# A cross-attention kernel: queries of batches 2 and 3 by seven block products, more warm-up products, and subtractions moved on Pool and VectorE

## Chip, core and metric

The kernel runs on one core of a Trainium2 chip. A core has a matrix engine (TensorE, PE in the profile, with its weight loads as PEld), VectorE (DVE), ScalarE (ACT), Pool (GpSimd) and SyncE (SP), which here only issues transfers. All data is float32. The metric is the device time of one launch in microseconds (us); the median of 3 runs before the change is 906.13 us (905.66 to 906.14). The profile is of one further execution, in the trace of which every instruction has a start and a duration.

## What is computed

For each of 16 batches there are 100 rows of hidden states `x` (640 wide, 8 heads of 80) and 722 rows of context (384 wide), of which the last 4 are tokens for a second attention. Cut to what matters:

```python
query = hidden_states @ Wq
keyt, valt = enc @ Wk, enc @ Wv              # enc: 718 context rows
hs = _mha(query, keyt, valt)                 # main attention
ca_q1 = jnp.einsum('btc,th->bch', ca, Wq_ca)[:, indices, :]
ca_hs1 = _mha(ca_q1, residual, residual)     # over the 100 rows of x
ca_q2 = ca_hs1 @ Wq
ca_hs2 = _mha(ca_q2, ca @ Wk_ca, ca @ Wv_ca) # over the 4 tokens
out = (hs + ca_hs2) @ Wout + b_out + residual
```

## The kernel before

The loop at the end of the kernel runs over the batches `b`. In batch b the values of b and the keys of b+1 are computed; the main attention of b and the second attention of b and b+1 run around them. The order on every engine is the program's order (a manual schedule), so an instruction waits in its engine's queue behind everything that the program issues to this engine before it.

**Values and keys** (`Values`, `Keys`, both from `Blocks`). The product of 3 x 3 blocks of context with 3 x 2 blocks of weights is made by 15 block products instead of 18, from sums of context blocks that Pool makes (`enc_sums`, L497). Each step of `vv.go(n)` or `kk.go(n)` issues n block products (L431 values, L462 keys) into banks of PSUM named A to E, and after each product reads the bank: the first time into a block of the output by a copy of ScalarE (L404), later by an addition of VectorE (L402). The next product into the same bank waits for that read. Bank C of the keys takes a place that bank C of the values must have left.

**Softmax of the main attention.** `scores` leaves three tiles `st[0]` to `st[2]`. `Maximum` finds row maxima in steps on VectorE (transposes, reductions) and spreads them into a tile `over`; `top.go(n)` takes n of its steps. `subtract(i)` (L1517, VectorE, two operands in SBUF, 120 x 1600) and `exponential(i)` (L1525, ScalarE) follow.

**The second attention** (`Second`). `scores1` makes `e1` on Pool, for each of 4 tokens a multiply (L980) and, from the second on, an addition (L987). `softmax1(n)` takes n steps of a `Maximum` over `e1`; with `fine` that maximum is cut into smaller steps; when all are taken and `hold` isn't set, VectorE subtracts (L1006). `scores2` ends with a subtraction of 100 x 32 elements on the engine it is given (L1062; VectorE in batch 1, Pool from batch 2 on). `softmax3` makes `p2` on Pool (L1076). `values2` makes, on Pool, for each token a multiply of the token's value row `vb` (L1091) and an addition (L1098); the transfers of the rows of tokens 2 and 3 are issued on SP after the multiplies of tokens 0 and 1 (two buffers).

**Queries.** Two batches share one product with `Wq`. `queries` (L541) does it plainly: for each of 5 chunks of 128 columns, 5 products of 128 x 128 weights with 200 columns. `Queries.make` does it for batches 4 and 5 and on: the fifth chunk plainly (L632), the first four as a 2 x 2 block product by seven block products instead of eight (L599), with remainders, into banks named a to f. Its first sums of inputs and weights are made on Pool by `Queries.sums` (L593, six subtractions), a further one in between (L656). They lie in the unused part of the context tile of batch b+2. Between the products `make` issues steps of the second attention's maximum (`between`), products of the fifth keys chunk (`chunk.go`, L742) and what is given in `steps`. It needs the block (1, 0) of `Wq` to hold the sum of two blocks, which VectorE makes in place (L1826) at the end of batch 1.

**Output.** The output rows are taken in tiles of 128 rows; some pairs of tiles are complete after batches 2, 5, 7, 10 and 12 (`PAIRS`, keyed by the batch). They are projected by `project_pair` (L1259) in the batch after, that is 3, 6, 8, 11 and 13, where `last.b in PAIRS`: the "output batches" below. There Pool adds the bias to the rows of `x` (L1133, two additions) and makes two sums (L1240), and VectorE reads the banks of the product (L1270). `MIXED` are the batches 3, 5, 7, 9, 11 and 13, in which the queries of the next pair are made by `Queries.make`.

**Start.** While the first data are loaded, 21 small products of a zero tile run on TensorE (L1333); the first real ones are `first_values` (L372).

## Time and profile before

| | us |
|---|---|
| median of 3 runs | 906.13 |
| the profiled execution, whole | 907.72 |
| its span (first to last instruction) | 906.0 |
| busy in the span: PE | 900.3 (99%) |
| busy: DVE | 720.6 (80%) |
| busy: POOL | 712.8 (79%) |
| busy: ACT | 461.9 (51%) |

Rows of the timeline have start, duration, engine, line of the kernel, operation, output and inputs, shape, the number of instructions merged into the row, and in brackets the idle time before it with what ended it. A product in float32 leaves two records. [...] Rows of a source line give minimum, median and maximum duration in ns.

### The profile page before, as it was taken

The numbers are of one execution on the slowest core, as the hardware profiler recorded it, in microseconds if no ns is written. First come the engines' busy times: TensorE is split into PE (matmuls) and PEld (weight loads), VectorE is DVE, ScalarE is ACT, GpSimd is POOL, SyncE is SP. The second block draws the span as 40 slices with busy tenths as digits, with TensorE's granted clock in tenths as the row PEclk, the third lists the DMA queues.
The fourth block names the chain that finished last, engine by engine and source line by source line (L and its number), as shares of the span: only waits on it lengthen the run. The fifth ranks groups of instructions, "written<-read, shape, count | busy, mean of one in ns | idle before, by whom it ended". The sixth has DMA issues, their size and how long they took to land.

```text
span 906.0 us, 28486 instructions
## 1 busy us (share of the span) xinstructions
PE 900.3 (99%) x12200; PEld 748.1 (83%) x12200; DVE 720.6 (80%) x1278; ACT 461.9 (51%) x917; POOL 712.8 (79%) x684
## 2 busy tenths in 40 slices
PE   9999999999999999999999999999999999999998
PEld 6898889787797878878798787988879788797866
DVE  3669796999849898786987869788984899848893
ACT  2344543747437564644737446375742747437451
POOL 8689998787868889696896959958897688976633
PEclk9999999999999999999999999999999999999999
DMA  8723111132301212230122301203130031310111
GB/s 292 264 70 92 36 58 43 37 95 53 112 4 52 80 41 67 54 105 32 53 56 53 106 34 52 56 25 107 54 83 32 24 107 53 98 32 24 62 47 38
DMA packets 50627, 63.00 MB, mean 70 GB/s; under 512 B 13594, under 2 KB 37850, under 8 KB 50500
## 3 DMA queue, kind: packets, MB, share of 16 engines
q1 hardware_dynamic: 48852, 59.18, 21.4%
q8 instruction: 96, 1.57, 0.7%
q10 hardware_dynamic: 1024, 1.15, 0.4%
q0 software_dynamic: 624, 0.85, 0.3%
q14 instruction: 31, 0.25, 0.1%
HBM read 55.59 MB, written 5.57 MB: 68 GB/s over the span
## 4 chain that ended last, share of the span: by engine, by line
PE 94%; DVE 5%; ACT 0%; DMA 0%; issue 0%; DVEq 0%
PE a_ps L1806 12%; PE s_ps L781 12%; PE v_psA L431 10%; PE k_psA L462 8%; PE v_psB L431 8%; PE k_psB L462 6%; PE o_ps L1259 5%; PE k_psA L742 4%; PE v_psC L431 3%; PE k_psC L462 3%; PE v_ps L372 2%; PE q_ps L599 2%; PE q_ps L541 2%; PE v_psD L431 2%; PE v_psE L431 2%; PE k_psE L462 1%
## 5 line engine op out<-in xcount | busy, mean ns | idle before, releaser
L980 POOL TENSOR_TENSOR e<-ca,g 100x800 f32<-100x800 f32 x64 | 97.9, 1540 | 90.9 <-ACT kT L404 67.4
L1806 PEld LDWEIGHTS a_ps<-vs,st 120*64 120x64 f32 (+3 forms) x3072 | 119.0, 124 | 10.1 <-issue 0.7
L497 POOL TENSOR_TENSOR enc<-enc 128x240 f32<-128x240 f32 x144 | 113.2, 796 | 14.2 <-DMA enc<-in_enct 7.2
L1806 PE MATMUL a_ps<-vs,st 120*64 120x81 f32 (+3 forms) x3072 | 122.8, 233 | 0.0
L1517 DVE TENSOR_TENSOR st<-st,over 120x1600 f32<-120x1600 f32 x48 | 116.6, 2431 | 0.0
L431 PE MATMUL v_psA<-wv_sb,enc 128*120 128x320 f32 x352 | 109.3, 433 | 0.0
L1098 POOL TENSOR_TENSOR hs<-hs,hs 100x640 f32<-100x640 f32 x48 | 94.8, 1975 | 3.8
L987 POOL TENSOR_TENSOR e<-e,e 100x800 f32<-100x800 f32 x48 | 93.4, 1945 | 3.8
L462 PE MATMUL k_psA<-enc,wk_sb 128*128 128x240 f32 x384 | 95.2, 371 | 0.2 <-DVE kT L402 0.2
L1091 POOL TENSOR_TENSOR hs<-vb,p 100x640 f32<-100x640 f32 x64 | 90.6, 1426 | 3.8 <-DMA vb<-va_d 1.5
L431 PE MATMUL v_psB<-wv_sb,enc 128*120 128x320 f32 x296 | 91.9, 433 | 0.0
L1525 ACT ACTIVATE st<-st 120x1600 f32<-120x1600 f32 x48 | 73.9, 1539 | 23.5 <-DVE st L1517 23.2
L462 PEld LDWEIGHTS k_psA<-enc,wk_sb 128*128 128x128 f32 x384 | 71.5, 190 | 16.4 <-issue 1.2
L431 PEld LDWEIGHTS v_psA<-wv_sb,enc 128*120 128x120 f32 x352 | 64.2, 183 | 25.0 <-DVE vs L402 0.5
L1529 DVE TENSOR_TENSOR most<-most,st 120x800 f32<-120x800 f32 x64 | 68.0, 1063 | 14.3 <-ACT st L831 13.2
L462 PE MATMUL k_psB<-enc,wk_sb 128*128 128x240 f32 x320 | 77.9, 366 | 0.0
L781 PE MATMUL s_ps<-qp,kT 64*56 64x100 f32 (+1 forms) x3072 | 73.3, 248 | 0.0
L431 PEld LDWEIGHTS v_psB<-wv_sb,enc 128*120 128x120 f32 x296 | 54.1, 183 | 21.8 <-DVE vs L402 0.4
L781 PEld LDWEIGHTS s_ps<-qp,kT 64*56 64x56 f32 (+1 forms) x3072 | 67.0, 130 | 5.5 <-issue 4.2
L837 ACT COPY st<-s_ps 120x800 f32<-120x800 f32 x64 | 49.8, 830 | 38.7 <-PE s_ps L781 38.5
L1166 ACT COPY hsT<-turned_hs 32x160 f32<-32x160 f32 (+7 forms) x244 | 67.7, 278 | 3.0
L462 PEld LDWEIGHTS k_psB<-enc,wk_sb 128*128 128x128 f32 x320 | 60.9, 190 | 7.9
(213 smaller groups left out, 1905.9 us busy)
## 6 DMA issues: line engine op xcount, KB each, us to landing
vb<-va_d SPq DMA_DIRECT2D x62, 250.0 KB
enc<-in_enct SPq DMA_DIRECT2D x30, 240.0 KB
enc<-in_enct SPq DMA_DIRECT2D x15, 360.0 KB
xT<-in_xt SPq DMA_DIRECT2D x8, 500.0 KB
rest<-in_enct SPq DMA_DIRECT2D x31, 120.0 KB
xn<-in_x SPq DMA_DIRECT2D x11, 320.0 KB
out<-xn SPq DMA_DIRECT2D x11, 320.0 KB
ca<-in_cas SPq DMA_DIRECT2D x16, 156.2 KB
```

What stands on the lines that cost most here:

```text
L431: nc.tensor.matmul(at[0][j][:KN, : H // 2], a_form(self.enc, f)[:, j * KN : (j + 1) * KN], wv_there.get(f, wv_sb[:, W_AT[f]]), start=first ...
L462: nc.tensor.matmul(at[:, i * KT : (i + 1) * KT], wk_sb[:, W_AT[f], i], a_form(self.enc, f), start=(first and i == 0), stop=last, skip_grou ...
L497: nc.gpsimd.tensor_tensor(out, left, right, op)
L781: nc.tensor.matmul(s_ps[at][k0:k1, cols], w, rhs, start=not begun & {(at, k) for k in range(k0, k1, 32)}, stop=last, skip_group_check=True,)
L980: first = nc.gpsimd.tensor_tensor(to, self.ca[:, t, :].unsqueeze(1).to_broadcast([S, NH, S]), g[:, :, t].unsqueeze(2).to_broadcast([S, NH, ...
L987: made = nc.gpsimd.tensor_tensor(e, e, to, ALU.add)
L1091: first = nc.gpsimd.tensor_tensor(to, self.vb[t][:S].rearrange("p (h d) -> p h d", h=NH), p2[:, :, t].unsqueeze(2).to_broadcast([S, NH, D] ...
L1098: nc.gpsimd.tensor_tensor(sums, sums, to, ALU.add)
L1517: return nc.vector.tensor_tensor(st[i], st[i], top.over[:KN].unsqueeze(1).to_broadcast([KN, 2, ROWS]), ALU.subtract,)
L1525: nc.scalar.activation(st[i], st[i], AF.Exp, scale=SCALE)
L1529: most_now = nc.vector.tensor_tensor(most[:KN], most[:KN], st[i][:, u], ALU.max)
L1806: nc.tensor.matmul(a_v[lo:hi, h % 4], st[i // 2][: KEYS[i], i % 2, h * S + lo : h * S + hi], block(i, h // 4)[: KEYS[i], h % 4], start=(i ...
```

## The change

- 28 small products at the start instead of 21.
- In batch 1 the second attention's `scores1` for batch 2 comes behind `scores2` of batch 1, for all four tokens, and the subtraction of `scores2` is on Pool as in the other batches.
- In batch 1 `values2` makes tokens 0 and 1 where it made all four; tokens 2 and 3 follow within the queries.
- The queries of batches 2 and 3 are made by `Queries.make`, without a keys chunk between its products; its `sums` stand on Pool behind the load of the bias; the in-place sum of `Wq` blocks moves to the end of batch 0; the maximum of batch 2's second softmax is taken in fine steps between the products instead of in one piece before them.
- In the output batches one `vv.go(1)`, a values product with VectorE's eviction, comes ahead of `subtract(0)` and `exponential(0)` instead of behind them, so that `subtract(0)` and `subtract(1)` stand next to each other on VectorE.

```diff
--- before.py
+++ after.py
@@ -626,7 +626,8 @@
             def add(bank, g, m):
                 nc.vector.tensor_tensor(q(g, m), full(bank), q(g, m), ALU.add)
 
-            chunk.go(2)
+            if chunk:
+                chunk.go(2)
             for ch in range(HC):
                 for k in (0, 64):
                     nc.tensor.matmul(
@@ -643,14 +644,16 @@
                 )
             between(2)
             steps[0]()
-            chunk.go()
+            if chunk:
+                chunk.go()
             self.product(a, w(0, 0), v(0, 0), True)
             nc.scalar.copy(q(0, 0), full(a))
             steps[1]()
             self.rest(c, 0, 0, True)
             self.product(c, w(0, 1), v(1, 0), False)
             add(c, 0, 0)
-            chunk.go()
+            if chunk:
+                chunk.go()
             between(1)
             self.product(a, self.w2, self.t2, False)
             nc.gpsimd.tensor_tensor(self.w2, w(0, 1), self.w2, ALU.subtract)
@@ -660,7 +663,8 @@
             self.product(e, w(1, 1), self.t4, False)
             nc.scalar.copy(q(1, 0), full(e))
             add(a, 1, 0)
-            chunk.go()
+            if chunk:
+                chunk.go()
             self.product(b, self.w3, self.t3, True)
             add(b, 1, 0)
             between(1)
@@ -997,7 +1001,7 @@
                     e1,
                     f"1_{self.b}",
                     after - 1 in PAIRS or after in PLAIN,
-                    after in (*MIXED, *PLAIN) or after - 1 in PAIRS,
+                    after in (1, *MIXED, *PLAIN) or after - 1 in PAIRS,
                 )
             if self.less:
                 return
@@ -1329,7 +1333,7 @@
     idle = small.tile([P, P], F32, tag="idle", name="idle")
     nc.vector.memset(idle, 0.0)
     idle_ps = psum("idle_ps")
-    for _ in range(21):
+    for _ in range(28):
         nc.tensor.matmul(
             idle_ps[:32, :32], idle[:, :32], idle[:, :32], start=True, stop=True
         )
@@ -1603,12 +1607,16 @@
                     nc.gpsimd.tensor_tensor(o, left, right, ALU.subtract)
             elif last.b - 1 in PAIRS:
                 nc.gpsimd.tensor_tensor(wout2[:, 0], wout2[:, 0], forms[0], ALU.add)
-            second.scores1(seen, range(T - 1))
+            if b > 1:
+                second.scores1(seen, range(T - 1))
             top.go(3)
             kk.go(3)
             vv.go(3)
-            now.scores2(nc.vector if b == 1 else nc.gpsimd)
-            second.scores1(None, range(T - 1, T))
+            now.scores2(nc.gpsimd)
+            if b > 1:
+                second.scores1(None, range(T - 1, T))
+            else:
+                second.scores1()
             now.load(behind=seen)
             last.load(seen)
             top.go(1)
@@ -1625,12 +1633,17 @@
             if last.b in PAIRS:
                 last.sums()
             later = range(T - 1, T) if b in MIXED or last.b in PAIRS else range(0)
+            if b == 1:
+                later = range(2, T)
             now.values2(None, range(T - len(later)))
             vv.go(2)
             kk.go(1)
+            if last.b in PAIRS:
+                vv.go(1)
             subtract(0)
             exponential(0)
-            vv.go(1)
+            if last.b not in PAIRS:
+                vv.go(1)
             subtract(1)
             vv.go(1)
             kk.go(2)
@@ -1652,6 +1665,9 @@
                 nc.gpsimd.dma_start(out=bias, in_=bout[0].partition_broadcast(P))
             if not mixed:
                 second_next, enc_next = loads()
+            if b == 1:
+                first_queries = Queries(p + 1, xT_at[0], enc_next[0])
+                first_queries.sums()
             if b + 2 < B:
                 m_next = load_m(b + 2)
             late = mixed and last.b not in PAIRS
@@ -1672,8 +1688,6 @@
                     )
             if not mixed and last.b in PAIRS:
                 now.values2(None, later)
-            if b == 1:
-                second.softmax1(8)
         else:
             room = enc_tile("spare").rearrange("p f k -> p (f k)")
             spare.extend(room[:, i * H : (i + 1) * H] for i in range(2))
@@ -1704,8 +1718,17 @@
         if b % 2 and b + 1 < B:
             xT, tiles = xT_at[0], queries_tiles(p + 1)
             if not mixed:
-                for n, get in enumerate((psum1, psumk, psum1, psumk, bank)):
-                    queries(p + 1, xT, tiles, n, get)
+                first_queries.make(
+                    tiles,
+                    None,
+                    lambda n=9: second.softmax1(n, True),
+                    (
+                        lambda: None,
+                        lambda: None,
+                        lambda: now.values2(None, later),
+                    ),
+                )
+                second.softmax1()
             else:
                 if last.b in PAIRS:
                     second.softmax1()
@@ -1822,7 +1845,7 @@
         if b + 2 < B:
             second_next.products()
             second_next.copy()
-        if b == 1:
+        if b == 0:
             nc.vector.tensor_tensor(
                 wq_block(1, 0), wq_block(1, 0), wq_block(1, 1), ALU.add
             )
```

## The prediction

> **What bounds the kernel now.** I read the chain of waits first, then the timelines by engine around every place that the change touches.
>
> ```profile
> PE 94%; DVE 5%; ACT 0%; DMA 0%; issue 0%; DVEq 0%
> ```
>
> TensorE (PE in the rows) carries 94% of the chain, so a product less is worth its own time and anything that makes TensorE wait costs in full. VectorE (DVE), ScalarE (ACT) and Pool count only where they are late. The places where TensorE waits today are few. Two of them matter here, in batch 1 and in batch 13:
>
> ```profile
> 113.03 1.24 PE L431 MATMUL v_psA<-wv_sb,enc 128*120 128x320 f32 x4
> 114.48 1.05 PE L462 MATMUL k_psA<-enc,wk_sb 128*128 128x240 f32 x4 [0.20 <-DVE kT L402]
> 115.55 1.08 PE L462 MATMUL k_psE<-enc,wk_sb 128*128 128x240 f32 x4
> 131.98 8.65 PE L541 MATMUL q_ps<-xT,wq_sb 128*128 128x200 f32 x50
> 140.56 0.43 PE L742 MATMUL k_psC<-enc,w_sums 128*64 128x120 f32 x4
> ...
> 772.77 0.97 PE L462 MATMUL k_psB<-enc,wk_sb 128*128 128x240 f32 x4
> 774.08 1.08 PE L462 MATMUL k_psC<-enc,wk_sb 128*128 128x240 f32 x4 [0.34 <-DVE vs L402]
> ```
>
> In batch 1 a values block is followed after 1.45 us (114.48 - 113.03) and the keys block behind it after 1.07. Undisturbed, the steps are 1.08 and 0.81, as batch 3 shows below (231.51 - 230.43, 232.32 - 231.51). TensorE lost 0.37 + 0.26 = 0.63 us waiting for VectorE. In batch 13 a keys block of 0.81 took 1.31, so 0.50 was lost. The plain queries of batches 2 and 3 take 140.56 - 131.98 = 8.58 us.
>
> **The change part by part.** All times are of the profiled execution, 907.72 us with a span of 906.0; it lies 1.59 above the median of 906.13, and I add the differences to the median.
>
> *Warm-up products.*
>
> ```profile
> 1.13 2.45 PE L1333 MATMUL idle_ps<-idle 128*32 128x32 f32 x42 [1.13 <-DVE idle L1330]
> 3.63 1.42 PE L372 MATMUL v_ps<-wv_sb,rest 128*120 128x320 f32 x2
> 7.25 0.77 PE L372 MATMUL v_ps<-wv_sb,rest 128*120 128x320 f32 x2
> ```
>
> 42 records (21 products) take 2.45 us, so 7 more take 0.8 and would end at 4.4 where real work now begins at 3.63. Two records of the first real product take 1.42 us against 0.77 at 7.25: until about then the array runs at half rate, and loads of weights still wait for data. Ends: 0 (the gap is filled by waits anyway) and +0.8; I take **+0.3**, because a delay before 7.25 shrinks by half when the rate doubles. [...]
>
> *The second softmax's subtraction in batch 1, from VectorE to Pool, and the score products behind it.*
>
> ```profile
> L1062 POOL TENSOR_TENSOR e<-s,mx x14: 238/243/249, 170.9 to 872.1; 100x32 f32<-100x32 f32 x14
> L1062 DVE TENSOR_TENSOR e<-s,mx x2: 1222/1249/1276, 74.1 to 110.8; 100x32 f32<-100x32 f32 x2
> ```
>
> VectorE loses an instruction of 1.25 us just ahead of its evictions; Pool gains 0.24. The 0.63 us of TensorE waiting should go, for the eviction that TensorE waited for at 114.48 (0.20 by the row's own count, the rest in the loads behind it) comes some 1.25 sooner. Bounds: 0 and -0.63.
>
> *Seven block products for eight.*
>
> ```profile
> 246.75 0.86 PE L599 MATMUL q_psA<-xT,wq_sb 128*64 128x100 f32 x16
> 247.43 1.20 PE L599 MATMUL q_ps<-xT,wq_sb 128*64 128x100 f32 x24
> ```
>
> In batch 3 one block product (16 records) takes 247.43 - 246.75 = 0.68 us, a remainder (8 records) half, 0.34. The new queries are the fifth chunk (a fifth of 8.58, 1.7), seven products (4.8) and four remainders (1.4): 7.9 us for 8.58, a gain of 0.7 if nothing is waited for. But three of the products need sums that Pool makes first, and this is where I expect the loss. Pool's queue of batch 1 now, with VectorE's subtractions beside it:
>
> ```profile
> 110.52 3.03 POOL L980 TENSOR_TENSOR e<-ca,g 100x800 f32<-100x800 f32 x2
> ...
> 127.51 2.50 POOL L1091 TENSOR_TENSOR hs<-vb,p 100x640 f32<-100x640 f32 x2
> 130.09 1.54 POOL L1098 TENSOR_TENSOR hs<-hs,hs 100x640 f32<-100x640 f32 x1
> ...
> 138.98 0.60 POOL L1652 DMA_DIRECT2D bias<-in_bout  x1
> ...
> 123.10 2.72 DVE L1517 TENSOR_TENSOR st<-st,over 120x1600 f32<-120x1600 f32 x1
> 130.44 2.88 DVE L1517 TENSOR_TENSOR st<-st,over 120x1600 f32<-120x1600 f32 x1
> ...
> L593 POOL TENSOR_TENSOR enc<-xT x12: 596/608/613, 240.6 to 791.3; 128x200 f32<-128x200 f32 x12
> L593 POOL TENSOR_TENSOR enc<-wq_sb x6: 1262/1268/1281, 241.9 to 789.5; 128x512 f32<-128x512 f32 x6
> ```
>
> A large subtraction of VectorE takes about 1.8 us alone (226.80 below); here it takes 2.88, because it begins at 130.44 and runs only once Pool's addition has ended at 131.63. The two exclude each other. After the change Pool starts the score products some 0.5 us later (it first does the 0.24 subtraction, which waits for VectorE), and since TensorE and VectorE are 0.63 ahead, the third subtraction comes before the addition of 130.09 instead of behind it and holds it for 1.7. The addition ends near 131.63 + 0.5 + 1.7 = 133.8. Behind it in Pool's queue stand the bias load (0.6), then the six sums, 4 x 0.61 + 2 x 1.28 = 5.0. The first weight sum, third in order, is there at 134.4 + 2 x 0.61 + 1.27 = 136.9, the second at 139.4, and its update (1.28) at 140.7. TensorE, at 131.35 after the fifth chunk's 1.7, one product, one remainder and one product, is at the first of them at 134.75 and waits 2.1 us. It waits again for the other two, and the queries end 0.68 + 0.34 + 0.68 = 1.7 after Pool's last sum, at 142.4 instead of 140.56: **+1.8**, whatever TensorE gained before. There is no keys chunk between these products to fill the gap, as there is in batch 3.
>
> Behind the queries VectorE has two copies of the maximum, two adds and the scores' subtraction before it can evict the keys chunk that TensorE goes on with; that subtraction can meet a Pool multiply of 1.25 (half of the 2.50 row). 0 to 0.8, taken **+0.5**. Batch 1 in all **+2.3**; bounds +0.1 (the third subtraction does not hold Pool) and +4 (one hold of 1.7 more).
>
> *Moved and costed at nothing.* The in-place sum of the query weights goes from the end of batch 1 to the end of batch 0, where VectorE idles 2.65 us for ScalarE; uncovered it would cost 1.0. Pool's later work in batch 1 (two value products, five key rows, the sums of the next context, the output weights' differences) shifts by some 8.5 us (0.5 + 1.7 + 5.0 + 1.3); before batch 2 Pool idles 6.24. The rest, some 2 us, makes batch 3's scores late; the exclusion could then slow the maxima by up to 1.5, which is in the range. SP's two loads of token values for tokens 2 and 3 are issued after the same multiplies as before and are used later.
>
> ```profile
> 99.03 0.99 DVE L1541 TENSOR_TENSOR most<-st 128x800 f32<-128x800 f32 x1 [2.65 <-ACT st L837]
> ...
> 162.37 3.04 POOL L980 TENSOR_TENSOR e<-ca,g 100x800 f32<-100x800 f32 x2 [6.24 <-ACT kT L404]
> ```
>
> *Batches 3, 6, 8, 11 and 13: an eviction ahead of the first large subtraction.* Batch 3 now:
>
> ```profile
> 222.41 3.67 DVE L1517 TENSOR_TENSOR st<-st,over 120x1600 f32<-120x1600 f32 x1
> 226.00 0.88 DVE L402 TENSOR_TENSOR vs<-v_psC,vs 120x320 f32<-120x320 f32 x2
> 226.80 1.81 DVE L1517 TENSOR_TENSOR st<-st,over 120x1600 f32<-120x1600 f32 x1
> 228.53 0.81 DVE L402 TENSOR_TENSOR vs<-v_psB,vs 120x640 f32<-120x640 f32 x1
> ...
> 221.35 3.05 POOL L1133 TENSOR_TENSOR xn<-xn,bias 128x640 f32<-128x640 f32 x2
> 226.14 0.73 POOL L1240 TENSOR_TENSOR sum<-hsT 128x256 f32<-128x256 f32 x1
> ...
> 223.96 1.24 PE L431 MATMUL v_psC<-wv_sb,enc 128*120 128x320 f32 x4
> 230.43 1.24 PE L431 MATMUL v_psB<-wv_sb,enc 128*120 128x320 f32 x4
> 231.51 0.97 PE L462 MATMUL k_psC<-enc,wk_sb 128*128 128x240 f32 x4
> 232.32 1.24 PE L431 MATMUL v_psA<-wv_sb,enc 128*120 128x320 f32 x4
> ```
>
> The first subtraction stands 3.67 us, until Pool's two additions end at 224.40. That is what makes TensorE wait in batch 13, since the eviction behind it frees the bank for the next keys block. With the eviction first, that wait goes (at most 0.5 in batch 13, and I allow as much for 11). But the block to be evicted starts at 223.96, so its eviction ends at about 225.7, VectorE idles until then, and the two subtractions come back to back. By then Pool, no longer held, is in its second sum (to 226.1). The first subtraction runs from 226.1 to 227.85. What happens between two adjacent subtractions batch 15 shows:
>
> ```profile
> 883.08 1.81 DVE L1517 TENSOR_TENSOR st<-st,over 120x1600 f32<-120x1600 f32 x1
> 884.81 2.90 DVE L1517 TENSOR_TENSOR st<-st,over 120x1600 f32<-120x1600 f32 x1
> ...
> 883.42 2.61 POOL L1091 TENSOR_TENSOR hs<-vb,p 100x640 f32<-100x640 f32 x1 [0.27 <-DMA vb<-va_d]
> ```
>
> Pool's multiply, waiting since 883.42, goes between them and ends 1.14 after the first; the second then ends 1.68 later. So in batch 3 the second ends at 227.85 + 1.14 + 1.68 = 230.7, and the values eviction behind it at 231.4 instead of 229.34 (228.53 + 0.81). TensorE wants that bank at 230.43: it had 1.1 us to spare, and now waits **1.0**. By the same walk over rows for which there is no room here, batch 8 has the same spacing (1.0) and batch 6 a little more room (0.7); in 11 and 13 the wait that goes about pays for the new one (0). Sum **+2.7**; bounds -1.0 (only the gain) and +9 (below).
>
> Then the third subtraction, two microseconds later than now, meets Pool's additions again, ahead of the read that frees a bank of the output product:
>
> ```profile
> 235.81 0.45 DVE L1270 TENSOR_TENSOR xn<-o_ps,xn 128x320 f32<-128x320 f32 x1
> 236.90 2.32 PE L1259 MATMUL o_ps<-wout,hsT 128*128 128x320 f32 x8
> ```
>
> The read ends 0.64 us before TensorE needs it. VectorE is 2.0 late, TensorE 1.0, so at least 0.4 is lost in batch 3, and 1.9 if a Pool addition (1.54) goes first. Over five batches 0 to 4; I take **+2.0**. Sum: 0.3 + 2.3 + 2.7 + 2.0 = +7.3, 906.13 to **913.4** (915.0 for an execution like the profiled one).
>
> [...]
>
> **The rivals.**
>
> [...]
>
> [...]
>
> *Pool is not held in these stretches, and the change gains.* This decides in batch 1, on Pool: TensorE comes to the product that needs the second weight sum at 134.75 + 0.68 + 0.34 + 0.68 = 136.45, so the six sums must begin by 131.4. Without holds of about 1.7 from three subtractions they would begin 5.1 sooner than 134.4, at 129.3, and nothing waits: -0.63 - 0.7 there. Without holds the five batches only gain their 1.0, and the total is 0.3 - 1.3 - 1.0 = -2.0: 904.1. Against it stand the rows 2.72 and 2.88 in this very stretch.
>
> **How the numbers follow.** About what a measurement of this kernel can tell from no change is 0.2%, 1.8 us: 904.3 to 907.9. The forecast has 0.61, with its own range 909 to 917 from the bounds of its terms; the slower rival 0.12; the one near 907.7 0.14; the faster one 0.13. Slower 0.73, same 0.14, faster 0.13. The range, 904.6 to 917, holds the forecast and the rival at 907.7 and leaves out the faster one and half of the slowest.
>
> **What would show it.** In batch 1: the pair of blocks at 113.03 steps at 1.08 and 0.81, and the query products show waits for Pool's sums, some 2 us ahead of the first weight sum. In batches 3, 6 and 8: two adjacent large subtractions, the second above 2.5 us with a Pool instruction between them, and TensorE waiting for a values eviction. In 11 and 13 the wait of the keys block is gone. I am wrong if the queries of batch 1 run 7.9 us without a gap, or if the values blocks of batches 3 and 8 keep their 1.08 steps.

## The result and the profile after

The changed kernel takes 920.69 us (median of 4 runs, 919.99 to 921.02). Its ratio to the kernel before is 1.016, 95% interval 1.0143 to 1.0178. The forecast was 913.4, from 904.6 to 917.0: slower, as forecast, but by twice as much. One part of the difference is the yardstick: 23 later runs of the kernel before have a median of 906.83 us and go from 905.90 to 909.01. Against this the change costs 13.9 us, and the spans of the two traces differ by 918.8 - 906.0 = 12.8.

The chain of waits of the kernel after, shares by engine:

```profile
PE 90%; DVE 7%; issue 2%; POOL 1%; DMA 0%; ACT 0%; ACTq 0%; POOLq 0%; DVEq 0%
```

TensorE has lost four points of the chain, VectorE has won two. What TensorE waited for, in the same trace (us in total, times, longest):

```profile
PE o_ps L1263 <- DVE xn L1274: 4.9, 5, 1.3
PE v_psB L431 <- DVE vs L402: 2.0, 5, 0.4
...
PE q_ps L599 <- ACT hsT L1189: 0.7, 1, 0.7
...
PE q_psA L599 <- POOL enc L593: 0.6, 1, 0.6
```

Five waits for an output read and five for a values eviction: one of each in every output batch. The reader can place the time by batches. From each trace I took the start of the first product of the second attention (`z_ps`), which every batch has, and the distance from one to the next; the table has the difference of these distances to the kernel before. Two of the experiments below stand beside it: e1_pairs (only the moved eviction) and e2_rest (all but that).

| stretch | forecast | after | e1_pairs | e2_rest |
|---|---|---|---|---|
| start and batch 0 | +0.3 | +0.19 | +0.46 | +0.31 |
| batch 1 | +2.3 | +1.84 | -0.27 | +2.44 |
| batch 2 | 0 | +1.13 | +0.01 | +1.12 |
| batch 3 | | +2.64 | +2.60 | 0.00 |
| batch 6 | | +1.55 | +1.55 | -0.17 |
| batch 8 | | +1.76 | +1.72 | +0.01 |
| batch 11 | | +2.25 | +2.25 | -0.38 |
| batch 13 | | +2.04 | +0.44 | -0.61 |
| these five | +4.7 | +10.24 | +8.56 | -1.15 |
| all others | 0 | -0.6 | -0.1 | 0.0 |
| span | +7.3 | +12.8 | +8.6 | +2.7 |

**Batch 1.** The timeline of the kernel after around the new queries, VectorE, Pool, TensorE:

```profile
129.90 2.15 DVE L1521 TENSOR_TENSOR st<-st,over 120x1600 f32<-120x1600 f32 x1
...
130.45 3.02 POOL L1102 TENSOR_TENSOR hs<-hs,hs 100x640 f32<-100x640 f32 x1
...
134.04 0.62 POOL L593 TENSOR_TENSOR enc<-xT 128x200 f32<-128x200 f32 x1
...
137.69 1.28 POOL L593 TENSOR_TENSOR enc<-wq_sb,enc 128x512 f32<-128x512 f32 x1
139.04 1.28 POOL L659 TENSOR_TENSOR enc<-wq_sb,enc 128x512 f32<-128x512 f32 x1
...
136.64 0.91 PE L599 MATMUL q_psA<-enc 128*64 128x100 f32 x16 [0.58 <-POOL enc L593]
...
139.02 0.91 PE L599 MATMUL q_psB<-enc 128*64 128x100 f32 x16 [0.44 <-POOL enc L593]
...
142.14 0.38 PE L746 MATMUL k_psC<-enc,w_sums 128*64 128x120 f32 x4
```

This is the walk of the prediction: the third subtraction goes ahead of Pool's addition, which takes 3.02 us in its row (130.45) for 1.54 in the kernel before (130.09); the six sums start at 134.04, TensorE waits for them, and the queries end at 142.14 (forecast 142.4), 1.8 us after Pool's last sum (139.04 + 1.28).

**Batch 2**, the maxima of the scores on VectorE beside Pool's differences of output weights:

```profile
157.66 2.11 DVE L1545 TENSOR_TENSOR most<-st 128x800 f32<-128x800 f32 x1 [2.69 <-ACT st L841]
159.87 4.41 DVE L1533 TENSOR_TENSOR most<-most,st 120x800 f32<-120x800 f32 x2
...
159.00 2.18 POOL L1607 TENSOR_TENSOR wout<-wout_sb 128x640 f32<-128x640 f32 x1
161.26 2.17 POOL L1607 TENSOR_TENSOR wout<-wout_sb,wout 128x640 f32<-128x640 f32 x1
```

Each maximum takes 2.1 to 2.2 us (two in the second row); in batch 2 of the kernel before the first takes 1.35 us (155.62) and the next two 2.02 together (157.62). Pool, late from batch 1, puts a difference between each two of them. I had given this as a bound of 1.5 and costed it at nothing.

**Batch 3**, the output batch that the prediction walked through:

```profile
228.81 2.14 DVE L1521 TENSOR_TENSOR st<-st,over 120x1600 f32<-120x1600 f32 x1
230.87 2.89 DVE L1521 TENSOR_TENSOR st<-st,over 120x1600 f32<-120x1600 f32 x1
233.68 0.81 DVE L402 TENSOR_TENSOR vs<-v_psB,vs 120x640 f32<-120x640 f32 x1
...
238.13 3.04 DVE L1521 TENSOR_TENSOR st<-st,over 120x1600 f32<-120x1600 f32 x1
...
242.03 0.45 DVE L1274 TENSOR_TENSOR xn<-o_ps,xn 128x320 f32<-128x320 f32 x1
...
229.23 2.85 POOL L1095 TENSOR_TENSOR hs<-vb,p 100x640 f32<-100x640 f32 x1
...
237.95 1.54 POOL L1102 TENSOR_TENSOR hs<-hs,hs 100x640 f32<-100x640 f32 x1
...
232.49 0.54 ACT L404 COPY kT<-k_psB 128x480 f32<-128x480 f32 x1
...
231.97 0.97 PE L462 MATMUL k_psA<-enc,wk_sb 128*128 128x240 f32 x4
233.08 1.08 PE L462 MATMUL k_psB<-enc,wk_sb 128*128 128x240 f32 x4
234.55 1.34 PE L431 MATMUL v_psB<-wv_sb,enc 128*120 128x320 f32 x4 [0.39 <-DVE vs L402]
...
238.42 2.85 PE L1263 MATMUL o_ps<-wout_sb,hsT 128*128 128x320 f32 x10
242.62 2.39 PE L1263 MATMUL o_ps<-wout,hsT 128*128 128x320 f32 x8 [1.35 <-DVE xn L1274]
```

A Pool multiply (229.23) goes between the two subtractions, the eviction ends at 234.49, and TensorE starts `v_psB` 2.58 us after `k_psA`, where two keys blocks of 0.81 make 1.62: 0.96 lost, as forecast. (A block is taken from the start of its row to the start of the next, for the rows overlap: in the kernel before, the one of 231.51 lasts 0.97 us and the next starts after 0.81.) The eviction ends last and sets this time, but 0.40 of it was lost ahead of that, at `k_psB`: it starts 0.30 late (233.08) and takes 0.1 longer, because ScalarE copies out the block before it in this bank (232.49 to 233.03) only behind `exponential(0)`, and this one waits for the first subtraction, which the change has made later. Then the third subtraction waits for Pool's addition of 237.95, the read ends at 242.48, and the output product goes on 4.20 us after it began, for ten records of 0.27, that is 2.69: 1.51 lost. The same two steps in batches 6, 8, 11 and 13 give 0.85, 0.96, 0.95, 0.96 and 0.61, 0.61, 1.50, 1.51. The first wait sums to 4.7 us (forecast 2.7), the second to 5.7 (forecast 2.0); 1.2 us of waits that the trace of before has in batches 6, 11 and 13 go. That makes 9.3 of the 10.2 us; the rest, some 0.2 a batch, lies in the products right behind the two waits.

### The profile page after: what moved, and what is told of

Same layout as the page of the kernel before. It is cut to its first block, busy times and chain, and to the rows that moved or that the text cites. A ratio compares the mean times of both kernels' runs of the same rounds, so it can differ in the third digit from the quotient of the medians.

```text
span 918.8 us, 28760 instructions
## 1 busy us (share of the span) xinstructions
PE 903.5 (98%) x12328; PEld 745.2 (81%) x12328; DVE 724.8 (79%) x1282; ACT 462.6 (50%) x917; POOL 714.1 (78%) x692
## 3 DMA queue, kind: packets, MB, share of 16 engines
q10 hardware_dynamic: 1024, 1.15, 0.4%
## 4 chain that ended last, share of the span: by engine, by line
PE 90%; DVE 7%; issue 2%; POOL 1%; DMA 0%; ACT 0%; ACTq 0%; POOLq 0%; DVEq 0%
PE a_ps L1829 12%; PE s_ps L785 12%; PE v_psA L431 10%; PE v_psB L431 8%; PE k_psA L462 8%; PE k_psB L462 6%; PE o_ps L1263 4%; PE k_psA L746 4%; PE v_psC L431 4%; DVE st L1521 3%; PE k_psC L462 2%; PE v_ps L372 2%; PE q_ps L599 2%; PE v_psD L431 2%; PE v_psE L431 2%
## 5 line engine op out<-in xcount | busy, mean ns | idle before, releaser
L497 POOL TENSOR_TENSOR enc<-enc 128x240 f32<-128x240 f32 x144 | 112.5, 791 | 12.8 <-DMA enc<-in_enct 5.7
L1095 POOL TENSOR_TENSOR hs<-vb,p 100x640 f32<-100x640 f32 x64 | 101.7, 1600 | 2.7 <-DMA vb<-va_d 0.2
L462 PEld LDWEIGHTS k_psB<-enc,wk_sb 128*128 128x128 f32 x320 | 60.4, 190 | 10.2 <-ACT kT L404 2.4
```

The lines of the kernel that those rows point to most:

```text
L462: nc.tensor.matmul(at[:, i * KT : (i + 1) * KT], wk_sb[:, W_AT[f], i], a_form(self.enc, f), start=(first and i == 0), stop=last, skip_grou ...
L497: nc.gpsimd.tensor_tensor(out, left, right, op)
L1095: first = nc.gpsimd.tensor_tensor(to, self.vb[t][:S].rearrange("p (h d) -> p h d", h=NH), p2[:, :, t].unsqueeze(2).to_broadcast([S, NH, D] ...
```

## The experiments

**The parts alone.** e1_pairs is the kernel before with this one edit of the diff:

```diff
+            if last.b in PAIRS:
+                vv.go(1)
             subtract(0)
             exponential(0)
-            vv.go(1)
+            if last.b not in PAIRS:
+                vv.go(1)
```

> The kernel before with only the eviction of one values product moved ahead of the first large subtraction in the five output batches (3, 6, 8, 11, 13). Theory A (this move alone makes nearly the whole loss; each output batch pays by itself, once where TensorE waits for a values eviction and once where it waits for the read of an output bank): the five batches grow by the 10.2 us by which they grew between the two traces, 906.1 + 10.2 = 916.3 us, from 915 to 917.5; TensorE's waits show five times some 0.4 for v_psB and five times some 1.0 to 1.3 for o_ps. Theory B (the forecast's size, first wait 2.7 and second 2.0): 910.8 us. Theory C (batch 1's new queries make Pool late, and it is that lateness that the output batches pay for): under 1 us of loss, 906 to 907.

Measured: 916.2 us, ratio 1.0103 (1.0090 to 1.0117). Theory A. But four batches pay both waits, not five, as TensorE's waits in its trace show:

```profile
PE o_ps L1259 <- DVE xn L1270: 3.6, 4, 1.3
PE v_psB L431 <- DVE vs L402: 1.6, 4, 0.4
```

Batch 13 is the exception, and it shows what sets the price:

```profile
780.41 2.17 DVE L1517 TENSOR_TENSOR st<-st,over 120x1600 f32<-120x1600 f32 x1
782.50 2.35 DVE L1517 TENSOR_TENSOR st<-st,over 120x1600 f32<-120x1600 f32 x1
...
789.23 1.81 DVE L1517 TENSOR_TENSOR st<-st,over 120x1600 f32<-120x1600 f32 x1
...
780.98 2.19 POOL L1240 TENSOR_TENSOR hsT<-sum,hsT 128x256 f32<-128x256 f32 x1
```

Here Pool was 0.9 later (its bias additions start 17.09 us into the batch, in batch 3 16.22), so that what went between the two subtractions was a sum of 0.7 us and not a multiply of 1.26: the second subtraction takes 2.35 for 2.89, the third meets no addition and takes 1.81, and TensorE doesn't wait for the eviction and loses only 0.28 at the read (the output product goes on 2.97 us after it began, 792.48 - 789.51, for 2.69). That is mostly why the two parts sum to 11.3 in span and the whole is 12.8: batch 13 pays 1.6 more in the whole than here.

e2_rest is the changed kernel with this hunk taken back.

> The changed kernel without that move: warm-up, order in batch 1, seven block products for batches 2 and 3. Theory A: the differences of the traces outside the five output batches remain, -0.15 at the start, +0.34 batch 0, +1.84 batch 1, +1.13 batch 2, -0.6 at the end and in batch 10, sum +2.6: 908.7 us; with the 1.8 us that the spans of the two traces do not explain, up to 910.5. Theory B (the forecast): +2.6 by another split, warm-up 0.3 and batch 1 2.3, 908.7 us, with batch 2 as before. Theory C: most of the loss: 916 or more.

Measured: 910.72 us, ratio 1.0039 (1.0027 to 1.0051), 0.2 above the upper end of theory A, with batches 1 and 2 as in the table: theory A by its split.

e3_warm28 is the kernel before with `range(28)` for `range(21)` at the start; e4_scores has the hunk of `scores1` and `scores2` alone (in batch 1 `now.scores2(nc.gpsimd)` and all four score products behind it).

> The kernel before with 28 small warm-up products for 21. Theory A (what the traces show, -0.15 us up to the scores of batch 0): 905.9 to 906.1 us. Theory B (the forecast, real work waits behind the added products): 906.4 us. Theory C (the whole 0.8 us of the added products): 906.9 us.

> The kernel before with only batch 1's order changed: the subtraction of the second scores on Pool for VectorE, and all four score products of batch 2 behind it. Theory A: the 0.63 us that TensorE waits around 114 us go, and the queries, still plain, ask for nothing from Pool: 905.5 us. Theory B: the gain is lost again before batch 2 starts, since Pool is 0.5 us later for what follows: 906.1 us or slightly more.

Measured: e3 907.24 us, ratio 1.0004 (0.9995 to 1.0012); e4 906.57 us, ratio 0.9993 (0.9984 to 1.0001). Neither differs from before by more than can be told. In e4's trace batch 1 is 0.74 us shorter, but so it is in that of e7_both below, which leaves batch 1 as it was, while in that of e6_read, which leaves it so too, it is as long as before; the wait at 114 us comes and goes.

**The first wait.** e5_hold adds to e1_pairs that Pool's value products start behind the second subtraction:

```diff
-            now.values2(None, range(T - len(later)))
+            if last.b not in PAIRS:
+                now.values2(None, range(T - len(later)))
...
-            subtract(1)
+            second_part = subtract(1)
+            if last.b in PAIRS:
+                now.values2(second_part, range(T - len(later)))
```

> e1_pairs (the move alone, +9.4 us) with Pool held out from between the two adjacent subtractions: in the output batches its first multiply with the value rows waits for the end of the second subtraction. Theory A (the first wait comes from the Pool multiply that goes between the two subtractions, 1.1 us, and nothing else): the second subtraction takes some 1.8 us for 2.89, TensorE's waits for v_psB go, the third subtraction comes 1.1 earlier but still meets a multiply; batches 3, 11 and 13 lose 1.2 us each for 2.6, batches 6 and 8 some 0.4 for 1.7: 906.8 + 4.4 = 911.2 us. Rival B (the adjacency itself is what costs: two subtractions of 1.75 us in front of the eviction, whatever Pool does): the v_psB waits stay at over half their size, 914 us or more. Rival C (Pool, held back, is late for everything behind it and the loss only moves): no faster than 916.

Measured: 909.61 us, ratio 1.0034 (1.0020 to 1.0047). Theory A, and more is won than it said. Batch 3 in its trace, with the third subtraction of batch 11 (672.32):

```profile
227.18 2.11 DVE L1517 TENSOR_TENSOR st<-st,over 120x1600 f32<-120x1600 f32 x1
229.21 1.81 DVE L1517 TENSOR_TENSOR st<-st,over 120x1600 f32<-120x1600 f32 x1
...
235.40 2.86 DVE L1517 TENSOR_TENSOR st<-st,over 120x1600 f32<-120x1600 f32 x1
...
672.32 1.81 DVE L1517 TENSOR_TENSOR st<-st,over 120x1600 f32<-120x1600 f32 x1
...
231.10 2.51 POOL L1091 TENSOR_TENSOR hs<-vb,p 100x640 f32<-100x640 f32 x2 [3.50 <-DVE st L1517]
...
239.70 2.39 PE L1259 MATMUL o_ps<-wout,hsT 128*128 128x320 f32 x8 [0.74 <-POOL hs L1098]
```

Pool idles 3.50 us for the subtraction, the second one takes 1.81, and no `v_psB` wait is left in any batch (in batch 13 a sum of Pool still goes between, and the second takes 2.35). So it was the Pool multiply between the subtractions, not their standing side by side, that made TensorE wait for the eviction. What ScalarE's late copy costs stays: `k_psB` begins 1.08 us after `k_psA` in batch 3 (231.42 - 230.34, for 0.81) and takes 0.1 longer, 0.37 in all, and as much in batches 8 and 11. It stays, at 0.3 to 0.5 us, in nearly every output batch of the runs with the moved eviction, and no run here was made to take it out.

The same trace shows what the second wait hangs on. In batch 3 the third subtraction still meets a multiply (2.86), and TensorE loses 0.91 at the read (the 0.74 is put down to Pool, but the read that frees the bank ended at 239.56, just before). In batches 6, 8 and 11 it meets nothing (1.81), and TensorE doesn't wait for a read; in batch 13 it takes 1.81 too, but starts later, and 0.28 is lost. Batch 3 is 1.34 longer than before, batch 6 0.25, batch 8 0.39, batch 13 0.29, and batch 11 as long as before.

**The second wait.** e6_read moves the third subtraction of e1_pairs behind the first read of an output bank, e7_both does so in e5_hold:

```diff
-            if not late:
+            if not late and last.b not in PAIRS:
                 subtract(2)
...
-                last.project_pair(lambda n: second.softmax1(n, True))
+                calls = []
+
+                def between(n):
+                    calls.append(n)
+                    if len(calls) == (2 if b in MIXED else 1):
+                        subtract(2)
+                        exponential(2)
+                    second.softmax1(n, True)
+
+                last.project_pair(between)
```

> e1_pairs with the third subtraction (and its exponential) behind the first read of an output bank for ahead of it, in the output batches. Theory A (the second wait, o_ps for the read, comes from the third subtraction that stands ahead of the read, longer and later than before): TensorE's waits for the read go, the v_psB waits stay; about 1.0 us a batch remains: 911.5 us. Rival B (VectorE is behind as a whole, so the next read or eviction is late instead): the wait goes to another row, 915 or more.

> e1_pairs with both: Pool held out from between the subtractions, and the third subtraction behind the first read. Theory A (these two waits are the whole cost of the move, and they add up): both waits go and the kernel is back at the time of before, 906.8 us within 1. Rival B (a third wait comes up in their place, in the exponentials or the sums for the queries, since Pool is later): 909 or more, and the waits of TensorE name its row.

Measured: e6 914.95 us, ratio 1.0094 (1.0079 to 1.0109); e7 913.63, ratio 1.0079 (1.0064 to 1.0094). Rival B both times, and e7 is slower than e5 without this edit. (In e6's trace batches 3 and 11 are 1.0 shorter than in e1_pairs, 6 and 8 hardly, and 13 is 0.7 longer.) The reads' line of TensorE's waits in e7:

```profile
PE o_ps L1259 <- DVE xn L1270: 4.5, 5, 2.1
```

The wait has gone from the first read to the third. Two more places were tried, both on e5_hold in batches 3, 11 and 13: e13_late has the third subtraction and its exponential behind `project_pair`, e14_third at the third call of `between`, behind the third read.

> e5_hold (+3.1 us) with the third subtraction and its exponential, in batches 3, 11 and 13, behind all of the output product for ahead of it. Theory A (what is left in these batches is the third subtraction ahead of the reads of the output banks, and e6_read and e7_both only moved it ahead of the next reads): the three batches are at 64.3 us, 906.45 + 0.7 for batches 6 and 8 = 907.2 us. Rival B (the subtraction is now late for the attention products or meets the sums for the queries): new waits of TensorE for st or for Pool's sums, 908.5 or more.

> e5_hold (+3.1 us) with the third subtraction and its exponential of batches 3, 11 and 13 behind the third read of an output bank, where VectorE waits for TensorE, and not behind the whole output product as in e13_late, where ScalarE's copies had to wait for it. Theory A (the third subtraction ahead of the first read is what is left of the loss in these batches): no wait of TensorE for a read, the three batches at 64.3 us, 906.4 + 0.7 (batches 6 and 8) = 907.1 us. Rival B (wherever it stands ahead of a read, some read is late, as in e6_read and e7_both): a wait of 0.5 or more a batch on the fourth read, 908.5 or more.

Measured: e13 930.07 us, ratio 1.0259 (1.0245 to 1.0273); e14 912.95, ratio 1.0064 (1.0052 to 1.0077). In e13 no read is late any more, but the exponential stands on ScalarE ahead of copies that TensorE needs, which I had overlooked (the mean granted clock of this execution is 0.989, see the last section):

```profile
PE k_psC L742 <- ACT kT L734: 14.9, 3, 5.0
```

In e14 the subtraction takes VectorE's gap and the fourth read comes late:

```profile
239.25 2.04 DVE L1517 TENSOR_TENSOR st<-st,over 120x1600 f32<-120x1600 f32 x1
...
242.64 1.29 DVE L1270 TENSOR_TENSOR xn<-o_ps,xn 128x320 f32<-128x320 f32 x3
...
243.28 1.85 PE L1259 MATMUL o_ps<-wout_sb,hsT 128*128 128x320 f32 x6 [1.31 <-POOL enc L593]
```

The product goes on 0.15 us after the read of 242.64 ended (0.49 of the row's three). So the wait doesn't hang on one order of two instructions: at each of the three places tried (behind the first read, behind the third, behind the whole product) the subtraction with its exponential made something else late. In the kernel before it stood two microseconds earlier, ahead of that stretch.

e16_all is e14_third with e4_scores.

> e14_third with batch 1's order of e4_scores as well. Theory A (the parts add up): e14_third less 0.5 us, 906.6 us. Rival B: the 0.74 us that batch 1 gained in the trace of e4_scores is given back elsewhere, and the two are equal.

Measured: 912.6 us, ratio 1.0060 (1.0047 to 1.0072), within the interval of e14: not decided.

**Batches 1 and 2.** All on e2_rest. e8_wout moves the three differences of output weights to the end of batch 2; e9_sums puts the sums of the new queries ahead of all value products of batch 1 (`later = range(T)`) and of the bias load; e11_novalues leaves these value products out, with zeros in place of their sum.

> e2_rest (910.7 us) with the three differences of output weights that Pool makes at the start of batch 2 moved to the end of batch 2. Theory A (batch 2 is 1.1 us longer because Pool, late from batch 1, makes these differences while VectorE takes the maxima of the scores): batch 2 is back at 46.8 us, 909.6 us in all, and the three maxima take 1.0 us each for 2.1 to 2.2. Rival B (something else that Pool is late with holds VectorE in batch 2): batch 2 stays at 47.9, 910.7 us. Rival C (the differences now come late for the first output product): batch 3 longer than 64.3.

> e2_rest (910.7 us) with Pool's sums for the new queries of batch 1 ahead of all four value products and of the bias load, which follow later. Theory A (the sums set the end of the queries in batch 1): the two waits of TensorE for Pool's sums (1.17 and 0.44 us by their rows, some 2.2 with what stands behind them) go and batch 1 takes 2.2 us less: 908.5 us; batch 2 keeps its +1.1, since Pool's work in sum is the same. Rival B (the queries wait for the transposed rows, by the 0.70 row, and then for VectorE's adds): less than 0.7 us gained, 910 us. Rival C (the value products come so late that the end of the batch waits for them): 911 or more.

> e2_rest (910.7 us) with the value products and additions of the second attention of batch 1 left out, so that Pool has 9.7 us less to do there. Theory A (Pool's amount of work between the scores and the end of batch 1 makes both the waits in the queries and the lateness in batch 2): the waits for Pool's sums (2.2 us in all) and for the keys chunk (0.4) go and batch 2 is at 46.8: 910.7 - 2.6 - 1.1 = 907.0 us, with the 0.70 us wait for the transposed rows left. Rival B (the new queries are slow by themselves, by their banks and reads): 909 us or more.

Measured: e8 912.0 us, ratio 1.0056 (1.0044 to 1.0069); e9 910.64, ratio 1.0045 (1.0028 to 1.0062); e11 907.11, ratio 1.0007 (0.9998 to 1.0015). In e8 batch 2 is back at 46.81 us, as theory A said, and batch 3 takes 3.05 more, since the differences now meet its maxima and hold everything behind them: rival C in another form. In e9 the queries run from 131.31 to 140.12, 8.8 us with one wait of 0.67 for the transposed rows, and no wait for a sum: the sums did set their end. Batch 1 is yet only 0.3 shorter than in e2 and batch 2 1.2 longer, because the value products have become what is late (at 149.06 VectorE has stood 2.94 us for Pool's last addition):

```profile
PE k_psA L746 <- DVE kT L736: 2.2, 1, 2.2
PE v_psA L431 <- DVE vs L402: 1.2, 1, 1.2
```

In e11 Pool has 9.7 us less to do, and batch 1 is 1.9 shorter than in e2 and batch 2 1.1: theory A, at 907.0 forecast and 907.11 measured. Pool's amount of work is the cause of these two losses, and moving it only moves the place. Even so batch 1 is 0.53 longer than in the kernel before: the waits for the transposed rows (0.7) and for one sum (0.4) are left.

e12_vsums gives the sums to VectorE and puts the transposes of the rows of batch 0 behind the new queries, e15_apart also makes Pool's last value products wait for the end of the sums.

> e2_rest (910.7 us) with the sums for the new queries of batch 1 on VectorE for Pool, and the transposes of the rows of batch 0 behind these queries for ahead of them. Theory A (seven products for eight gain 0.7 us where nothing has to wait for Pool): no wait within the queries, batch 1 takes 55.2 us (55.86 in e4_scores less 0.7), batch 2 is at 46.8: 905.4 us, below the kernel before. Rival B (VectorE, with 2.3 us more to do, is late for the adds of the queries or the maximum behind them): 906.5 to 908.

> e12_vsums (915.2 us) with Pool's products of the last two value tokens of batch 1 waiting for the end of VectorE's sums. Theory A (each sum on VectorE took up to 1.8 us because a Pool instruction went between each two of them): the sums take 0.4 to 0.8 us each, the 3.4 us wait for them goes, batch 1 takes 55.2 to 56.5 us for 65.2, and the kernel is at 905.5 to 907 us. Rival B (VectorE is simply too late with its maximum and the adds of the queries): batch 1 stays above 60 us, 910 or more.

Measured: e12 915.22 us, ratio 1.0098 (1.0082 to 1.0113); e15 909.03, ratio 1.0028 (1.0019 to 1.0037). The first sums in e12:

```profile
134.18 1.82 DVE L594 TENSOR_TENSOR enc<-xT,enc 128x200 f32<-128x200 f32 x1
135.92 2.02 DVE L594 TENSOR_TENSOR enc<-wq_sb 128x512 f32<-128x512 f32 x1
...
138.08 1.33 PE L600 MATMUL q_psA<-enc 128*64 128x100 f32 x16 [3.39 <-DVE enc L594]
```

and in e15:

```profile
134.16 0.37 DVE L594 TENSOR_TENSOR enc<-xT,enc 128x200 f32<-128x200 f32 x1
134.44 0.69 DVE L594 TENSOR_TENSOR enc<-wq_sb 128x512 f32<-128x512 f32 x1
...
135.28 0.91 PE L601 MATMUL q_psA<-enc 128*64 128x100 f32 x16 [0.75 <-DVE enc L594]
```

The same two instructions take 0.37 and 0.69 us without Pool and 1.82 and 2.02 with it. Yet batch 1 is at 59.00 us in e15, not at the 55.2 to 56.5 of theory A: the waits that are left (0.75 for a sum, 0.66, 0.80 and 0.52) are for VectorE, which is late with everything. The seven products themselves are as short as forecast (8.81 us in e9 with one wait of 0.67 and what hangs on it), but that one wait already makes them longer than the plain 8.58, and no kernel has a shorter batch 1 with them.

## Why the prediction was wrong

**The direction, batch 1 and the first wait of batch 3 were right**, by their own rows: +2.3 forecast, +1.84 and +2.44 measured for batch 1, 1.0 and 0.96 for the wait. e9 shows that Pool's sums set the end of the queries, e5 that the Pool multiply between the two subtractions makes the eviction late. Two waits were missing from the forecast, and both lie in the shadow of these: the one for the transposed rows in batch 1 (0.67 at 134.81) and the one for ScalarE's copy in the output batches (0.40 of the 0.96). The rival near 907.7, in which VectorE makes both subtractions with no Pool instruction between them, is refuted by the 2.89 row, and the one in which nothing is held by batch 1.

**The step that failed most** is "Over five batches 0 to 4; I take +2.0" for the third subtraction and the read behind it. It measured 5.7. I had written that TensorE loses at least 0.4 in batch 3, and 1.9 if a Pool addition goes first. The 2.0 is five times the 0.4; five times the 1.9 is 9.5, so the case with the addition was neither in the value nor inside its bound of 4. That case came, in all five batches: the third subtraction takes 3.04 or 3.05 us in each, with the addition ahead of it. It cost 1.5 in batches 3, 11 and 13, where a step of the second attention's maximum (1.00 us at 241.10) stands between the subtraction and the read, and 0.6 in 6 and 8, where the read comes first (409.47, right behind the subtraction of 406.50). e5 shows the condition: without a Pool instruction ahead of it the subtraction takes 1.81, and at most 0.28 is lost. A term that repeats under one condition is five times the one price or five times the other, and the range must hold both.

**The second** is "in 11 and 13 the wait that goes about pays for the new one (0)". The new wait is 0.95 there as in batch 3, where I had set it against 0.5; what went was 0.38 and 0.61, the shares of before's waits in these batches. Over the five batches the first wait is 4.7 and the waits that went are 1.2, so 3.5 for the 2.7 of the sum. I took Pool's place in these batches from the rows of before. But its bias additions start 16.24 us into batch 11 after the change (665.40 less the batch's first `z_ps` at 649.16) and 16.90 before it (657.19 less 640.29); with 0.66 us more its sums are done in time and the multiply stands between the subtractions, as in batch 3. e1_pairs shows how little decides it: in batch 13, with the additions at 17.09, a sum goes between, and TensorE doesn't wait for the eviction. The steps behind the waits, 1.0 in sum, were not in the forecast at all.

**The third** is batch 2, "Moved and costed at nothing": 1.1 us, inside the bound of 1.5 that I gave. Pool's delay was worked out as 8.5 us less the 6.24 for which it idles. But it comes to the first of the three differences 6.4 us later than before (157.37 for 150.99) while the batch begins 2.0 later, and the 6.24 stand behind the differences (at 162.37), so they took nothing off. The differences, which before were done ahead of all but the first maximum, now fall on the maxima; e8 moves them, and the maxima are back at 0.99 and at 2.02 for two.

**The warm-up** (+0.3) was -0.15 in the trace, +0.30 in e2's, and nothing that can be told in e3. No run shows that a delay at the start shrinks by half, as the term has it; the first two records of real work took 1.42 us at 3.63 before and 0.80 at 4.11 after. What the spans leave open (14.6 us between the first medians, 12.8 between the traces) is the yardstick: I added the differences to 906.13, while the trace is of an execution of 907.72 and 23 later runs have a median of 906.83.

The slower rival, 919.6 with 1.25 more for a second Pool instruction at each second subtraction, came near the time for a wrong reason. No run shows this term, on which the +9 of the first wait's range rests too: the second subtraction took 2.89 us in each of the five batches of after, with one multiply between, and the first wait sums to 4.7; in the five batches Pool never took two turns while a subtraction waited. Two waits a batch did it. No version here is faster than the kernel before by more than can be told.

## What to carry to other kernels

Where instructions of two engines hold each other up (here VectorE's large subtraction, 1.81 us in e5_hold and 2.89 in the changed kernel with a Pool multiply ahead of it), an instruction moved next to its like on one engine opens a slot for the other between them, so price a move by what stands ready on the other engine, and follow the lateness to every later deadline of that engine, not only to the next. Where a pattern repeats in several stages, a cost that hangs on one condition is there in most of them or in hardly any: forecast the sum with the condition and without it, and don't put the lower price into the sum. And a saving on the engine that sets the end is nothing when it is bought with work on an engine whose queue is already full to the next deadline.

## What the runs showed of the hardware

A waiting instruction does not always get its turn when the other engine's instruction ends. In e8_wout a large subtraction of 1.8 us took 4.32, through both bias additions of Pool, as in the 3.67 row of before (222.41), and in batches 11 and 13 of before (4.32 and 4.33 us):

```profile
227.43 4.32 DVE L1521 TENSOR_TENSOR st<-st,over 120x1600 f32<-120x1600 f32 x1
...
227.03 3.04 POOL L1137 TENSOR_TENSOR xn<-xn,bias 128x640 f32<-128x640 f32 x2
```

It is not fixed for this pair: in batch 6 of before the subtraction (388.33, 1.99 us) went between the same two additions, which then took 4.64 us together from 387.09. In batch 13 of e7_both the longer wait happened with another pair of Pool instructions:

```profile
786.80 3.60 DVE L1517 TENSOR_TENSOR st<-st,over 120x1600 f32<-120x1600 f32 x1
...
786.50 1.53 POOL L1098 TENSOR_TENSOR hs<-hs,hs 100x640 f32<-100x640 f32 x1
788.00 0.72 POOL L1279 TENSOR_TENSOR hsT<-hsT,hsT 128x256 f32<-128x256 f32 x1
```

Pool's multiplies back to back let VectorE in between them in batch 3 of the change (229.23 and 232.04, 5.67 us for the two together, where the second subtraction came before the next multiply). So one engine got two instructions in a row against a waiting one in some rows, and only one in others. What decides it wasn't tried.

With 21 warm-up products the first two records of real work took 1.42 us (before, e1_pairs, e4_scores, e5_hold, e6_read and e13_late, at 3.57 to 3.63), about twice as long as later ones (0.70 to 0.80). When this ended differed from one execution of the same start to the next: the first row of two records at 0.80 or less begins at 6.49 to 7.43 us in five of these traces, and in e5_hold the row of 7.71 still takes 1.27; the start took 1.50 us more than before there. With 28 it begins at 4.11 and 4.14 (after, e3_warm28) and 5.36 (e2_rest, e8_wout), and in e9_sums the first two records, at 4.26, still take 1.42. Where it came early, TensorE then waited 0.62 and 0.81 us for weights that were still being loaded (after at 6.07, e3_warm28 at 6.29), and no gain of the 28 can be told (ratio 1.0004 in e3_warm28).

Products were slower behind some waits within the kernel, too. In e13_late a record of `k_psC`, 240 columns, took 0.66 us right behind the wait of 4.99 us (251.82), in e14_third, at 248.49, 0.37; the mean granted clock of the execution was 0.989. In e12_vsums the block product behind the wait of 3.39 us took 1.06 from its start to the next (139.14 - 138.08), in e15_apart, behind 0.75, it took 0.70 (135.98 - 135.28); the mean granted clock was 0.996. The executions of e7_both and e9_sums, whose longest waits behind the start are 2.1 and 2.2 us, have a mean of 1.0. So the losses of e12 and e13 hold more than the waits themselves.
